# Layer-norm transposes moved from TensorE to VectorE blocks and an exchange through DRAM

## The chip, the cores and the metric

The kernel runs on one core of a Trainium2 chip. The core has five engines that work side by side, each through its own instructions in order: TensorE (PE in the profile; PEld is its weight load), VectorE (DVE), ScalarE (ACT), GpSimd (POOL) and SyncE (SP), which here only issues DMAs. An engine waits on semaphores that other engines and DMAs raise. The metric is the device time of one execution in microseconds (us), the median of several runs.

## The reference

The input is eight sequences `x` of 512 tokens and 128 features, all in float32. Three steps follow one another, each added to `x`: half an FFN of the layer-normed `x`, attention over the layer-normed `x`, half an FFN of the layer-normed `x` again, with the same FFN weights.

```python
x = x + 0.5 * ffn(layernorm(x))
x = x + attention(layernorm(x))      # 16 heads, rank 64, softmax over 512 keys, V*O folded into VO
x = x + 0.5 * ffn(layernorm(x))

def ffn(h):
    for blk in range(3):
        y = qlora_linear(h, 2 * blk)              # 128 -> 128
        y = layernorm(y) * gamma[blk] + beta[blk]
        y = gelu(y)                               # exact gelu
        h = qlora_linear(y, 2 * blk + 1) + h
    return h
```

So each sequence goes through nine layer norms over the 128 features: one in front of each FFN, three inside each FFN, and one in front of the attention. The quantized weights and their low-rank parts are folded into one 128 x 128 matrix per layer (`wT`) at the start.

## The kernel before

A tile holds one sequence as [128 tokens, 4 chunks, 128 features]. A layer norm needs its statistics along the features, so it works with tokens on partitions; the matmul behind it contracts over features, so its input must have features on partitions. Between the two lies a transpose of each 128 x 128 chunk.

The order of work is written out by hand. A function `at(t, fn)` files each step under a time on a schedule, and at the end all steps are sorted by these times and recorded; that order is then the order on each engine. The times only order the work; they are not microseconds. The schedule is cut into 32 turns (`SUP` is 32.0 units of it, about 32 us on the chip); turn `s` is numbered from 0, and each does the scores and softmax of two pairs of heads. Four turns are one sequence's attention. The FFN steps of other sequences are woven into the turns.

In a turn, `lay_turn` handles eight chunks of scores (two pairs of heads by four query chunks), numbered 0 to 7 here. For each chunk TensorE writes the scores into one of two PSUM buffers tagged `scores` (line 752), VectorE takes the row maxima (line 759, called max0 to max7 below), ScalarE takes the exponentials and their sums (line 764), VectorE the reciprocal (line 771), GpSimd divides the first head (line 776) and ScalarE the second (line 778), and VectorE turns the result in 32 x 32 blocks (line 792). When four chunks are done, 16 DMAs issued from SP (line 848) move the blocks between partition groups, 2 MB in all, into `eT`, and TensorE multiplies `eT` with the values in the next turn (line 869). Two such exchanges are issued in each turn. Since there are two score buffers, the scores of chunk n+2 wait for the exponentials of chunk n. At the end of a turn come the projections (`pqk`, line 689), the values (`pv`, line 712) and the second matmuls of the FFN blocks (`po`, line 419). All of these stand on TensorE in the written order.

A layer norm is a `Norm` object with four steps: `stats` on VectorE (lines 352 and 354), `root` on GpSimd, which raises variance plus epsilon to the power -1/2 (line 360), `scale` on VectorE, four instructions of 128 x 128 that subtract the mean and multiply with the root (line 365), and `turn`, four transposes on TensorE into a PSUM bank (line 334). ScalarE then reads that bank: `gelu` inside an FFN block (line 412), a plain copy `ffn_start` in front of an FFN (line 431) or `keep` in front of the attention (line 620). Names in the profile: `z`, `mv`, `rstd` and `p` belong to the norms in FFN blocks; with `_n` to the norm in front of an FFN, with `_an` to the one in front of the attention.

How many norms fall into a turn follows from the schedule. From turn 7 to turn 26 the pattern repeats every four turns. In turns 7, 11, 15, 19 and 23 there are three (the attention norm, a block's norm and an FFN's first norm); in the other turns of that stretch there are two. In turns 8, 10, 12 and so on (the even ones) both belong to FFN blocks; in turns 9, 13, 17, 21 and 25 one is a block's and one an FFN's first.

In each turn the three `root`s and then, from schedule time 4.0 on, the divisions of line 776 stand on GpSimd, and VectorE holds max0, max1, then the `scale`s and two reciprocals, then max2.

Of the kernel before, what the change touches and what calls it, by code (L numbers as in the profile page):

```python
# [10 lines left out]
F32 = mybir.dt.float32  # L11
I32 = mybir.dt.int32
AF = mybir.ActivationFunctionType
# [5 lines left out]
def kernel(  # L19
# [26 lines left out]
    nc = tc.nc  # L46
    B, T, D = x.shape
    H, R, _ = wq.shape
    NL = qweights.shape[0]
    NB = NL // 2  # L50
    NG = scales.shape[2]
    GROUP = D // NG
    LR = lora_a.shape[1]
    P = 128
    NC = T // P
    Q4 = P // 32
    EPS = 1e-5
    HP = H // 2
    SUP = 32.0
# [3 lines left out]
    const = ctx.enter_context(tc.tile_pool(name="const", bufs=1))  # L63
    work = ctx.enter_context(tc.tile_pool(name="work", bufs=3))
    small = ctx.enter_context(tc.tile_pool(name="small", bufs=8))

    class Psum:


        def __init__(self):  # L70
            self.names, self.stack = ["start", "attention", "end"], ExitStack()
# [34 lines left out]
    xs = [const.tile([P, NC, D], F32, name=f"x{b}") for b in range(B)]  # L106
# [7 lines left out]
    G = 3  # L114
# [1 line left out]
    qk_sb = work.tile([P, 2, HP, D], F32, tag="eT", name="qk_sb", bufs=3)  # L116
    q_sb, k_sb = qk_sb[:, 0, :, :], qk_sb[:, 1, :, :]
    sc = const.tile([P, NL, NG], F32, name="sc")
    la = [const.tile([LR, G, D], F32, name=f"la{i}") for i in range(2)]
    lb = [const.tile([P, G, LR], F32, name=f"lb{i}") for i in range(2)]  # L120
    bias_rows = const.tile([NL, D], F32, name="bias_rows")
    gb_rows = const.tile([2 * NB, D], F32, name="gb_rows")
# [16 lines left out]
    def load_projections(g0, g1):  # L139
# [24 lines left out]
        out=bias_bc,  # L164
        in_=biases.rearrange("(k two) d -> two k d", two=2)[0].partition_broadcast(P),
# [8 lines left out]
    def at(t, fn, *args):  # L174
        tasks.append((t, len(tasks), fn, args))
# [34 lines left out]


    sc75 = const.tile([P, NL, NG], F32, name="sc75")
    w = [const.tile([P, G, NG, GROUP], F32, name=f"w{i}") for i in range(2)]
    lbT = [const.tile([LR, G, P], F32, name=f"lbT{i}") for i in range(2)]
    wT = const.tile([P, NL, P], F32, name="wT")

# [122 lines left out]
    class Norm:  # L339


        def __init__(self, src, name, tag):
            self.src, self.name, self.tag = src, name, tag

        def stats(self):

# [14 lines left out]

        def scale(self):
            z = work.tile([P, NC, D], F32, tag="z", name=f"z_{self.name}")
            for c in range(self.n):
                nc.vector.tensor_scalar(  # L365
                    z[:, c, :], self.src[:, c, :], self.mv[:, c, 0:1],
                    self.rstd[:, c : c + 1],
                    ALU.subtract, ALU.mult,
                )
            self.z = z[:, : self.n, :]  # L370

        def turn(self):
            self.p = transposed(self.z, f"p_{self.name}", self.tag)


    hTs = {}

    class Block:


        def __init__(self, f, k, b, tag):
            self.k, self.b, self.tag, self.name = k, b, tag, f"{f}_{k}_{b}"

        def first(self):
            self.py = bank(f"py{self.name}", self.tag)
# [6 lines left out]
        def biased(self):  # L392
            y = work.tile([P, NC, D], F32, tag="y", name=f"y{self.name}", bufs=2)
            nc.vector.tensor_tensor(  # L394
                y, self.py, bias_bc[:, self.k, :].unsqueeze(1).to_broadcast([P, NC, D]), ALU.add
            )
            self.norm = Norm(y, self.name, self.tag)
            self.norm.stats()

        def root(self):  # L400
# [5 lines left out]
        def turn(self):  # L406
            self.norm.turn()

        def gelu(self):
            k = self.k  # L410
            self.aT = work.tile([P, NC, P], F32, tag="aT", name=f"aT{self.name}", bufs=2)
            nc.scalar.activation(
                self.aT, self.norm.p, AF.Gelu,
                bias=gb[:, NB + k : NB + k + 1], scale=gb[:, k : k + 1],
            )

# [11 lines left out]

    def ffn_start(n, f, b):
        hTs[b] = work.tile([P, NC, P], F32, tag="hT", name=f"hT{f}_{b}", bufs=3)  # L430
        nc.scalar.copy(hTs[b], n.p)

    def ffn_add(f, b, tag):
        ph = transposed(hTs[b], f"ph{f}_{b}", tag)
# [135 lines left out]
    class Unit:  # L570


        def __init__(self, f, b):
            self.f, self.b, self.tag = f, b, f"g{f}"
            self.n = Norm(xs[b], f"n{f}_{b}", self.tag)

        def lay_start(self, times, tag=None):

            if tag:
                self.tag = self.n.tag = tag  # L580
            for at_n, (fn, *args) in zip(times, (
                (self.n.stats,), (self.n.root,), (self.n.scale,), (self.n.turn,),
                (ffn_start, self.n, self.f, self.b),
            )):
                at(at_n, fn, *args)

        def lay_blocks(self, s, i, other={}):

            for k in range(NB):
                m = Block(self.f, k, self.b, self.tag)
                for x, fn in zip(other.get(("first", k)) or T_FIRST[s % 4][i], (
                    m.first, m.biased, m.root, m.scale
                )):
                    at(s * SUP + x, fn)
                s += 1  # L600
                for x, fn in zip(other.get(("second", k)) or (
                    17.65 + 0.1 * i, 22.0 + 0.1 * i, 26.0, 25.4 + 0.8 * i, 26.3 + 0.8 * i
                ), (m.turn, m.gelu, exp_again, m.second, m.add)):
                    if x:
                        at(s * SUP + x, fn)
            at(
                s * SUP + other.get("end", 31.5 if s % 4 == 0 else 28.8),
                ffn_add, self.f, self.b, self.tag,
            )


    xTs, accs = {}, {}

    def lay_attn_input(b, t):

        n = Norm(xs[b], f"an{b}", "g0")

        def keep():
            xTs[b] = work.tile([P, NC, P], F32, tag="xT", name=f"axT{b}", bufs=2)
            nc.scalar.copy(xTs[b], n.p)  # L620

        at(t - SUP + 29.3, n.stats)
        at(t + 0.2, n.root)
        at(t + 4.7, n.scale)
        at(t + 17.65, n.turn)
        at(t + 17.8, keep)


# [19 lines left out]
        ),  # L648
    )

    T_EARLY, T_LATE = (28.9, 29.7, 32.3, 35.6), (31.4, 32.0, 33.8, 36.0)
    T_FIRST = (
        (T_EARLY, None), (T_EARLY, (24.2, 25.0, 26.8, 35.5)), (None, T_EARLY),
        ((25.5, 26.5, 28.5, 35.5), T_EARLY), (T_EARLY, T_LATE),
    )
    class Pair:

# [470 lines left out]
    for b in range(B):  # L1128
        if b:
            lay_attn_input(b, (b * Q - 1) * SUP)  # L1130

        if b > 2:
            s = (b - 1) * Q - 1
            t = s * SUP
            m = Unit(0, b)
            m.lay_start((t - 5.0, t + 1.1, t + 16.58, t + 20.3, t + 20.7))
            m.lay_blocks(s, 0)

        if b < B - 1:
            s = (b + 1) * Q + 1  # L1140
            t = s * SUP
            m = Unit(1, b)
            m.lay_start((t + 0.1, t + 1.1, t + 4.7, t + 17.65, t + 17.85))
            m.lay_blocks(s, 1, {
                ("second", 1): (17.75, 21.8, None, 43.2, 43.3),
                ("first", 2): (44.4, 45.45, 46.0, 46.4),
                ("second", 2): (27.80, 27.90, None, 30.44, 32.75),
                "end": 33.56,
            } if b == B - 2 else {})
# [136 lines left out]
```

## Time and profile before

| | |
|---|---|
| median of 3 runs | 1071.47 us (1070.93 to 1071.54) |
| span of the profiled execution | 1068.9 us, 2.6 us under that median; the rest lies around the span |
| PE busy | 1053.8 us, 99% of the span |
| DVE, ACT, POOL busy | 82%, 74%, 45% |
| granted TensorE clock | 0.9 or more of full speed in every slice |
| DMA | 142.4 MB; HBM reads 5.01 MB, writes 2.10 MB |
| four transposes of one norm on TensorE | 4 x 279 ns busy; they overlap |
| `scale` on VectorE, one instruction | 356 ns (`z`), 466 ns (`z_n`), 500 ns (`z_an`) |
| division on GpSimd, 128 x 512 | 1564 ns |
| block transpose on VectorE, 128 x 1024 | 1231 ns |
| one DMA of the exchange, 128 KB | 2.3 us from issue to landing, SP spends about 0.59 us on its issue |
| store of a result, 256 KB to DRAM | 2.4 us from issue to landing |

A busy PE row says only that some matmul is in flight. The chain that ended last and the timeline of each engine tell which wait ends last; they are shown with the prediction. Idle time of VectorE, ScalarE or GpSimd counts only where that engine's result is waited for.

### The profile page before, as it was taken

Reading aid. Unit: us, or ns where it says so; the run is one execution under the profiler, and the core shown is the slowest. Engines: PE = TensorE matmul, PEld = TensorE weight load, DVE = VectorE, ACT = ScalarE, POOL = GpSimd, SP = SyncE. Lnnn points to the kernel's source line nnn. Section 1 sums busy time; section 2 is a strip of 40 time slices with the busy share of each in tenths; the row PEclk is TensorE's granted clock in tenths of the full one; section 3 lists DMA queues with packets and bytes.
Section 4 is the critical chain, followed back from the end, with each engine's and each line's share of the span. In section 5 each row is a group of like instructions: output and inputs, shape, how many; then the busy total and the mean of one; then the engine's idle time right before and its main releaser. Section 6 shows DMA issues by size and latency. Waiting matters only on the chain.

```text
span 1068.9 us, 15650 instructions
## 1 busy us (share of the span) xinstructions
PE 1053.8 (99%) x4628; PEld 560.2 (52%) x4628; DVE 873.2 (82%) x1767; ACT 793.9 (74%) x1710; POOL 485.1 (45%) x368
## 2 busy tenths in 40 slices
PE   9899999999999999999999999999999999999998
PEld 7445554545555554555545555554555554455546
DVE  6897868788888888888889888888888888777765
ACT  4877787777777787777787777787777787777742
POOL 4554434545443454444445444455444445444423
PEclk9999999999999999999999999999999999999999
DMA  6166655665576555566455566555567555566660
GB/s 189 38 141 138 158 129 132 140 141 128 120 167 158 121 117 119 129 158 158 110 130 126 122 155 155 131 124 122 117 152 167 126 125 117 131 145 158 158 158 21
DMA packets 58572, 142.40 MB, mean 133 GB/s; under 512 B 18732, under 2 KB 22904, under 8 KB 58488
## 3 DMA queue, kind: packets, MB, share of 16 engines
q1 hardware_dynamic: 56120, 139.94, 57.0%
q10 hardware_dynamic: 2368, 1.45, 0.6%
q8 instruction: 39, 0.64, 0.3%
q14 instruction: 45, 0.37, 0.1%
HBM read 5.01 MB, written 2.10 MB: 7 GB/s over the span
## 4 chain that ended last, share of the span: by engine, by line
PE 91%; DVE 3%; ACT 2%; SPq 2%; issue 1%; DMA 0%; POOL 0%; DVEq 0%; ACTq 0%; POOLq 0%
PE acc L869 37%; PE ps L752 20%; PE pqk L689 10%; PE pv L712 10%; PE po L419 4%; PE py L387 4%; PE p L334 2%; ACT e L764 2%; PE py L489 1%; SPq L848 1%; DVE tr L792 1%; DVE nm L759 1%; SPq L824 1%; PE sum L835 1%; PE p_n L334 1%; PE ph L334 1%
## 5 line engine op out<-in xcount | busy, mean ns | idle before, releaser
L776 POOL TENSOR_SCALAR e<-e,rden 128x512 f32<-128x512 f32 x257 | 399.5, 1564 | 336.1 <-DVE rden L771 336.1
L764 ACT ACTIVATE e<-ps,nm 128x512 f32<-128x512 f32 x512 | 345.0, 685 | 157.5 <-DVE nm L759 151.5
L869 PE MATMUL acc<-eT,v 64*128 64x512 f32 (+1 forms) x1756 | 457.8, 590 | 0.7 <-DMA eT<-tr 0.7
L759 DVE TENSOR_REDUCE nm<-ps 128x2 f32<-128x1024 f32 x256 | 299.6, 1206 | 47.9 <-PE ps L752 47.7
L792 DVE STREAM_TRANSPOSE tr<-e 128x1024 f32<-128x1024 f32 x252 | 307.8, 1231 | 29.9 <-POOL e L776 21.9
L869 PEld LDWEIGHTS acc<-eT,v 64*128 64x128 f32 (+1 forms) x1756 | 192.2, 187 | 216.9 <-issue 215.1
L752 PE MATMUL ps<-qk 64*128 64x512 f32 x1024 | 248.1, 598 | 2.8 <-ACT e L764 1.8
L778 ACT ACTIVATE e<-e,rden 128x512 f32<-128x512 f32 x255 | 176.0, 726 | 15.2 <-DVE rden L771 13.9
L752 PEld LDWEIGHTS ps<-qk 64*128 64x128 f32 x1024 | 94.6, 186 | 126.2 <-issue 83.3
L712 PE MATMUL pv<-vo_sb,axT 128*128 128x256 f32 x512 | 121.7, 380 | 0.3 <-ACT e L764 0.3
L712 PEld LDWEIGHTS pv<-vo_sb,axT 128*128 128x128 f32 x512 | 94.8, 190 | 28.7 <-issue 12.4
L360 POOL TENSOR_TENSOR rstd<-mv,mhalf 128x4 f32<-128x4 f32 x42 | 42.9, 1022 | 146.7 <-DVE mv L354 145.9
L764 ACT ACTIVATION_READ_ACCUMULATOR e<-ps,nm 128x1 f32 x512 | 103.6, 202 | 0.0
L725 ACT COPY v<-pv 128x512 f32<-128x512 f32 x124 | 66.8, 594 | 42.0 <-PE pv L712 42.0
L771 DVE RECIPROCAL rden<-den 128x2 f32<-128x2 f32 x256 | 41.4, 165 | 36.3 <-ACT e L764 35.4
L695 ACT COPY qk<-pqk 128x1024 f32<-128x1024 f32 x61 | 61.0, 1000 | 3.9 <-PE pqk L689 3.9
L689 PE MATMUL pqk<-axT,qT_w 128*128 128x512 f32 x122 | 63.3, 601 | 0.2 <-ACT e L764 0.2
L689 PE MATMUL pqk<-axT,kT_w 128*128 128x512 f32 x122 | 62.3, 592 | 0.0
L387 PEld LDWEIGHTS py<-wT,hT 128*128 128x128 f32 x336 | 42.3, 191 | 13.0 <-DVE hT L425 9.2
L365 DVE TENSOR_SCALAR z<-y,mv,rstd 128x128 f32<-128x128 f32 x168 | 48.1, 356 | 0.6 <-POOL rstd L360 0.6
L394 DVE TENSOR_TENSOR y<-py,bias_bc 128x512 f32<-128x512 f32 x42 | 28.7, 683 | 22.6 <-PE py L387 22.0
L387 PE MATMUL py<-wT,hT 128*128 128x128 f32 x336 | 45.4, 278 | 1.0 <-DVE hT L425 0.8
(143 smaller groups left out, 724.0 us busy)
## 6 DMA issues: line engine op xcount, KB each, us to landing
eT<-tr SPq DMA_DIRECT2D x1008, 128.0 KB, 2.3
x<-in_L_attn_x_dram SPq DMA_DIRECT2D x7, 256.0 KB, 6.0
out_dram<-x SPq DMA_DIRECT2D x7, 256.0 KB, 2.4
eT<-tr SPq DMA_DIRECT2D x16, 64.0 KB, 2.0
eT<-tr ACTq DMA_DIRECT2D x16, 64.0 KB, 2.1
qk_sb<-in_L_attn_Q_dram SPq DMA_DIRECT2D x1, 448.0 KB, 4.4
qk_sb<-in_L_attn_K_dram SPq DMA_DIRECT2D x1, 448.0 KB
x<-in_L_attn_x_dram SPq DMA_DIRECT2D x2, 128.0 KB, 2.8
```

The lines of the kernel that those rows point to most:

```text
L387: nc.tensor.matmul(self.py[:, c, :], lhsT=hTs[self.b][:, c, :], rhs=wT[:, 2 * self.k, :], start=True, stop=True,)
L689: nc.tensor.matmul(self.pg[:, i, :], lhsT=(qT_w, kT_w)[i][:, self.g, :], rhs=xTs[self.b], start=True, stop=True,)
L695: nc.scalar.copy(self.qk, self.pg)
L712: nc.tensor.matmul(p, lhsT=xTs[self.b][:, c, :], rhs=vo_sb[:, 2 * self.g : 2 * self.g + 2, :], start=True, stop=True,)
L725: nc.scalar.copy(self.v[:, c : c + NC // 2], self.pv[:, c : c + NC // 2])
L752: nc.tensor.matmul(ps[:, j, :], lhsT=self.qk[rows, 0, ts(c, P)], rhs=self.qk[rows, 1, :], start=True, stop=True,)
L759: nc.vector.tensor_reduce(self.nm[:, c, :], self.ps[c], AX.X, ALU.max, negate=True)
L764: nc.scalar.activation(e[:, j, :], self.ps[c][:, j, :], AF.Exp, bias=self.nm[:, c, j : j + 1], accum_out=self.den[:, c, j : j + 1],)
L776: nc.gpsimd.tensor_scalar(e, e, r, None, ALU.mult)
L778: nc.scalar.activation(e, e, AF.Copy, scale=r)
L792: nc.vector.transpose(self.tr[:, :, :, c, :], self.e[c].rearrange("p h (k j r) -> p j (h k) r", j=Q4, r=32),)
L869: nc.tensor.matmul(accs[self.b][i], lhsT=self.v[rows, k, j, :], rhs=self.eT[rows, :, j * NC + k, :], start=first, stop=end and (j == 1 or ...
```

## The change

Of the 63 norms of this kind, 59 take a new way; four keep the old one (both first norms and the first block's norm of the earliest work, and the last norm before the end part).

- `scale` moves from VectorE to GpSimd, as four instructions of the same shape. It is filed just behind its `root`, so that on GpSimd it stands in front of the turn's divisions.
- `turn` on TensorE goes. In its place `spread` on VectorE turns the whole [128, 512] tile in 32 x 32 blocks, one instruction, into a tile `zout` that the norms of a turn share. It stands behind the first reciprocal of the turn; for the attention norm behind the second one. All of them stand in front of max2.
- Once per turn an `Exchange` runs on SP: one DMA writes `zout` to a DRAM tile `far` (256 KB per norm), and four DMAs read it back into `zin`, one per group of 32 partitions, in pieces of 512 bytes per norm. On SP it is filed between the two exchanges of `eT` (schedule time 6.0), and its reads wait for the write to have landed. There are 30 such exchanges.
- ScalarE's three readers take `zin` in SBUF where they took a PSUM bank.
- `zout` and `zin` share a buffer of one (`zx`). To make room, the setup's `la` and `w` tiles now live in that buffer before the first exchange.

```diff
+SPREAD = (4.2, 4.3, 5.45)
 class Norm:
     def scale(self):
         z = work.tile([P, NC, D], F32, tag="z", name=f"z_{self.name}")
+        engine = nc.gpsimd if self.exchange else nc.vector
         for c in range(self.n):
-            nc.vector.tensor_scalar(
+            engine.tensor_scalar(
                 z[:, c, :], self.src[:, c, :], self.mv[:, c, 0:1],
                 self.rstd[:, c : c + 1],
                 ALU.subtract, ALU.mult,
             )
...
+    def spread(self):
+        nc.vector.transpose(
+            self.exchange.out()[:, :, self.slot, :, :],
+            self.z.rearrange("p c (j r) -> p j c r", r=32),
+        )
+
+    def turned(self):
+        if self.exchange:
+            return self.exchange.landed[:, :, self.slot, :, :].rearrange("p i c q -> p c i q")
+        return self.p.rearrange("p c (i q) -> p c i q", q=32)
+
+class Exchange:
...
+    def tile(self, name):
+        return work.tile(
+            [P, Q4, self.n, NC, 32], F32, tag="zx", name=f"{name}{self.s}", bufs=1
+        )
...
+    def run(self):
+        f = self.n * NC * 32
+        far = dram.tile([P, Q4, f], F32, tag="far", name=f"far{self.s}")
+        nc.sync.dma_start(out=far, in_=self.sent.rearrange("p j a c q -> p j (a c q)"))
+        self.landed = self.tile("zin")
+        for j in range(Q4):
+            nc.sync.dma_start(
+                out=self.landed[32 * j : 32 * (j + 1)].rearrange("p i a c q -> p i (a c q)"),
+                in_=far.rearrange("(i r) j f -> j r i f", r=32)[j],
+            )
+
+def exchange_of(s):
+    if s not in exchanges:
+        x = exchanges[s] = Exchange(s)
+        at(s * SUP + 6.0, x.run)
+    return exchanges[s]
...
 def lay_attn_input(b, t):
-    n = Norm(xs[b], f"an{b}", "g0")
+    n = Norm(xs[b], f"an{b}", "g0", exchange_of(b * HP // 2 - 1))
...
     at(t + 0.2, n.root)
-    at(t + 4.7, n.scale)
-    at(t + 17.65, n.turn)
+    at(t + 0.3, n.scale)
+    at(t + SPREAD[2], n.spread)
     at(t + 17.8, keep)
...
-T_EARLY, T_LATE = (28.9, 29.7, 32.3, 35.6), (31.4, 32.0, 33.8, 36.0)
+T_EARLY, T_LATE = (28.9, 29.7, 32.3, 32.4), (31.4, 32.0, 33.8, 33.9)
...
-    m.lay_start((t + 0.1, t + 1.1, t + 4.7, t + 17.65, t + 17.85))
+    m.lay_start((t + 0.1, t + 1.1, t + 1.2, t + SPREAD[1], t + 17.85))
```

## The prediction

> **What bounds the kernel now.** I read the page's busy shares first, then the chain that ended last, then the timelines of one period of four turns (turn 15 starts at 499.7 us, 16 at 532.0, 17 at 564.2, 18 at 595.8).
>
> ```profile
> PE 1053.8 (99%) x4628; PEld 560.2 (52%) x4628; DVE 873.2 (82%) x1767; ACT 793.9 (74%) x1710; POOL 485.1 (45%) x368
> ...
> PE 91%; DVE 3%; ACT 2%; SPq 2%; issue 1%; DMA 0%; POOL 0%; DVEq 0%; ACTq 0%; POOLq 0%
> ...
> L776 POOL TENSOR_SCALAR e<-e,rden 128x512 f32<-128x512 f32 x257 | 399.5, 1564 | 336.1 <-DVE rden L771 336.1
> L360 POOL TENSOR_TENSOR rstd<-mv,mhalf 128x4 f32<-128x4 f32 x42 | 42.9, 1022 | 146.7 <-DVE mv L354 145.9
> L365 DVE TENSOR_SCALAR z<-y,mv,rstd 128x128 f32<-128x128 f32 x168 | 48.1, 356 | 0.6 <-POOL rstd L360 0.6
> ```
>
> TensorE carries 91% of the chain: it bounds the whole. GpSimd's 336 us of idle time wait for VectorE's reciprocals, so it has room on average. What matters is when. The chain's pieces at the end of turn 16, with ScalarE's timeline there and one row of the waits:
>
> ```profile
> 549.35 1.02 PE p L334 x8
> 550.38 3.44 PE acc L869 x8
> 553.81 1.72 PE pqk L689 x4
> 555.53 1.73 PE pv L712 x8
> 557.25 1.72 PE po L419 x4
> ```
>
> ```profile
> 555.89 1.45 ACT L412 ACTIVATE aT<-p,gb 128x512 f32<-128x512 f32 x2
> ```
>
> ```profile
> PEld po L419 <- ACT aT L412: 6.8, 22, 1.0
> ```
>
> Eight transposes (two norms) hold the chain for 1.02 us. But `po` behind them needs ScalarE's gelus: the first ends near 556.67 and `po` starts at 557.25, and 22 of the `po` weight loads already wait for them. The reader is to see that TensorE can't come forward by the whole 1.02 us. Next GpSimd and VectorE at the start of turn 15 (three norms):
>
> ```profile
> 499.11 1.03 POOL L360 TENSOR_TENSOR rstd_an<-mv_an,mhalf 128x4 f32<-128x4 f32 x1 [7.31 <-DVE mv_an L354]
> 500.88 1.01 POOL L360 TENSOR_TENSOR rstd<-mv,mhalf 128x4 f32<-128x4 f32 x1 [0.73 <-DVE mv L354]
> 501.86 1.01 POOL L360 TENSOR_TENSOR rstd_n<-mv_n,mhalf 128x4 f32<-128x4 f32 x1
> 504.96 1.58 POOL L776 TENSOR_SCALAR e<-e,rden 128x512 f32<-128x512 f32 x1 [2.09 <-DVE rden L771]
> ```
>
> ```profile
> 503.68 1.11 DVE L365 TENSOR_SCALAR z<-y,mv,rstd 128x128 f32<-128x128 f32 x4
> 504.77 1.84 DVE L365 TENSOR_SCALAR z_an<-x,mv_an,rstd_an 128x128 f32<-128x128 f32 x4
> 506.24 2.33 DVE L759 TENSOR_REDUCE nm<-ps 128x2 f32<-128x1024 f32 x2
> ...
> 517.10 1.19 DVE L365 TENSOR_SCALAR z_n<-x,mv_n,rstd_n 128x128 f32<-128x128 f32 x4
> ```
>
> GpSimd's last root of the turn ends at 502.87, and max2 starts at 506.24: 3.4 us for all that is now put on GpSimd between them.
>
> **The cost of one scaling on GpSimd (c).** The trace has no such instruction there. The nearest is line 776: the same operation on 512 columns in 1.56 us with one arithmetic step and one scalar. A quarter of it is 0.39 us, the lower bound. With a fixed part of 0.19 us (GpSimd's 128x1 additions, 190 ns each) the slope is 2.68 ns a column, and 128 columns take 0.53 us. If the second arithmetic step costs as much as the first, it is 0.19 + 2 x 0.34 = 0.88 us, the upper bound. I take 0.53, as the row is the same operation and the fixed part is measured.
>
> The Trainium skill speaks against the move: GPSIMD Engine Reference, section Engine selection, says to leave elementwise work on a tile to VectorE, since GpSimd is about half as fast; its section on elementwise accounting, however, gives 769 ns for 512 one-input elements, half of the 1564 ns that this trace shows. A quarter of the page's figure would make an estimate of c = 0.19 us and, by the walk below, of 1068 us for the whole (the turns of three norms then lose 0.4 us each, the others gain 0.3); no row here shows such a speed, and the row decides.
>
> **The change part by part.**
>
> *TensorE.* 59 norms x 4 transposes leave. In the chain view one norm holds 0.44 to 0.59 us: 1.47 us in a turn of three, 1.02 for two block norms, 0.93 for a block and a first norm. Over all turns 5 x 1.47 + 11 x 1.02 + 5 x 0.93 + 3 x 1.0 + 6 x 0.5 = 29 us. How much arrives depends on the wait behind it.
>
> *VectorE.* Four scalings per norm go (1.1 to 1.9 us), one block transpose of 512 columns comes: half of 1231 ns is 0.62, the 128x512 addition takes 0.68; I take 0.64. VectorE gets lighter, but all `spread`s stand in front of max2, and a `spread` waits for GpSimd. Behind it on VectorE are queued max2 and max3, behind these ScalarE's exponentials 2 and 3, and behind these TensorE's scores 4 and 5.
>
> *Turns of three norms (7, 11, 15, 19, 23), at turn 15's times.* GpSimd does the attention root, the block's root (ends 501.89), eight scalings, the last root (1.02, and 0.1 for its own result), four scalings: it ends at 501.89 + 12 x 0.53 + 1.12 = 509.37. The first `spread` in VectorE's order takes just that last result. Three of them and a reciprocal (0.12) put max2 at 509.37 + 3 x 0.64 + 0.12 = 511.41 instead of 506.24, 5.17 later. Scores 5 had 0.8 us of air (exponentials 3 end at 510.2, TensorE reaches them at 511.07), so TensorE stalls. Of the delay, 1.1 us come back where `z_n` no longer stands in front of max6 (517.10), and 0.28 us are added by two ScalarE reads from SBUF (line 778 from SBUF 726 ns, line 725 from PSUM 594: 0.13 to 0.14 each). `po` started 0.14 us behind its gelu (ends 525.48, starts 525.62), so there is no air: it comes 5.17 - 1.1 + 0.28 = 4.35 us later. The transposes' 1.47 us vanish in that wait. Five turns: +21.8 us.
>
> *Turns with a block and a first norm (9, 13, 17, 21, 25).* At turn 17's times GpSimd starts at 564.04: root, scalings, root, scalings end at 564.04 + 1.03 + 0.1 + 2.12 + 1.02 + 0.1 + 2.12 = 570.53; one `spread` and a reciprocal later max2 is at 571.29 instead of 570.71. `po` is bound by its gelu here too, so +0.58 + 0.14 = 0.72 us; five turns: +3.6.
>
> *Turns with two block norms (2, 8, 10, ... 26, eleven).* Their statistics are ready before the turn's scores (root at 531.41 in turn 16; scalings end by 534.6, max1 only at 535.45). No delay. The gain is `po`'s air: 557.25 - 556.67 less 0.1 for the semaphore and 0.14 for the SBUF read, 0.34 us; eleven turns: -3.7.
>
> *The rest.* Turn 1 has a division in front of its second norm on GpSimd, and max2 goes from 65.47 to 68.5: +3.0. Turn 27: GpSimd ends 889.83, max2 at 891.23 instead of 889.94, +1.4 with the gelu. Turns 3, 5, 6, 28 to 31: between 0 and -0.5 each, I take -0.2: -1.4.
>
> *DMAs and SP.* 59 x 256 KB go out and come back, +30 MB to 142. The write is issued when SP has issued its last `eT` (about 506 in turn 15) and `spread` is done: 511.4. The 256 KB store lands in 2.4 us; 768 KB at the 210 GB/s that the exchange reaches take 2.5 us more: landed at 516.3. The four reads take 0.6 us of SP each, 3.7 us of moving, 2.3 us to land: about 522.3. The copy that wants them stands in front of exponentials 6, now near 523.7, so it needs them by 522.9. It just fits. In turn 17 they land near 581.5 against 582.2. In the other turns they have 4 us. On SP the next 16 issues of `eT` stand behind the reads, but their tiles are ready later still (517.1, now 522.3). So: nothing, if the reads land as the rows say. Loads of 256 KB from DRAM at the start took 4.6 us in the median (6.3 at most); at 6.3 for the last read they would be 1 to 1.5 us late in ten turns, about 12 us.
>
> *The sum.* 21.8 + 3.6 + 3.0 + 1.4 - 3.7 - 1.4 = +24.7 us on the profiled execution's 1068.9, and so on the median that stands 2.6 above it: 1071.5 + 24.7 = **1096 us**, 2.3% slower. Each 0.1 us of c moves it by 12 x 5 + 8 x 7 scalings, 11.6 us: c = 0.39 gives 1080, c = 0.88 gives 1137.
>
> **The rivals.**
>
> *Two steps cost double on GpSimd* (c near 0.88): the same waits, longer: 1137 us (1120 to 1145). For it: one `root` of only four columns takes 1.02 us, so arithmetic isn't cheap there. Against: a power is no multiplication.
>
> *The data come late through DRAM.* The forecast plus 12 us: 1108. For it: the copy in front of exponentials 6 has half a microsecond of air. Against: DMA engines are idle from 507 to 517 us.
>
> *TensorE's saving arrives in full, and the kernel is faster.* If the gelu's chain can be shifted with TensorE, 29 us come off. Against it stand the late max2s, counted on TensorE alone: 5 x (5.17 - 0.5) + 2.5 + 0.8 = 26.7 us at c = 0.53, so 1069; at c = 0.39, 10.6 less, 1059. It decides from c of about 0.53 downwards. For it: 91% of the chain is TensorE's. Against: `po` already waits for its gelus. I give 1064.
>
> **How the numbers follow.** The forecast with c between 0.45 and 0.65 (1088 to 1110) gets 0.58; the lower end, c near 0.39 (1078 to 1086), 0.08; doubled cost 0.12; late data 0.10; TensorE's saving in full 0.12, of which 0.09 faster and 0.03 within 0.2%, which is about what a measurement can tell from no change here. So slower has 0.88. The range leaves out the faster part and the upper half of the doubled cost: 1072 to 1130.
>
> **What would show it.** Right: in turns 7, 11, 15, 19 and 23 VectorE's block transpose of `z` idles some 4 to 5 us for GpSimd's scaling, max2 comes 5 us late and TensorE's scores 4 and 5 wait for ScalarE; `po` waits more for `aT`; scalings on GpSimd near 0.53 us; TensorE's idle time rises from near nothing to over 40 us. Wrong: scalings under 0.3 us, `spread`s that never wait, or readers of `zin` that wait for DMAs. I would be wrong most of all by the price of that one instruction, or if ScalarE's chain to the gelu isn't as rigid as I read it.

## The result and the profile after

| | before | after |
|---|---|---|
| median | 1071.36 us (1070.93 to 1071.54, 4 runs) | 1132.92 us (1131.36 to 1133.40, 4 runs) |
| ratio, 95% interval | | 1.0573 (1.0558 to 1.0588) |
| span of the profiled execution | 1068.9 us | 1131.6 us |
| DMA | 142.4 MB | 173.3 MB |

The changed kernel is 5.7% slower; 1096 us was forecast, with 1130 us as the upper end. The direction was right, the size was not, and the range missed the time by 3 us. Line numbers in what follows are those of the changed kernel: the division of line 776 is now line 846, the scaling 372, the spread 383, scores 822, exponentials 834, the block's gelu 476, `po` 483.

From the page of the changed kernel, three parts: busy time of the engines, the chain by engine, and the group of the moved scaling (its busy time, mean ns of one, idle time before).

```profile
PE 1057.8 (93%) x4392; PEld 540.7 (48%) x4392; DVE 845.8 (75%) x1590; ACT 793.1 (70%) x1710; POOL 668.0 (59%) x604
...
PE 50%; DVE 14%; POOL 12%; ACT 10%; SPq 7%; issue 4%; DMA 3%; DVEq 0%; ACTq 0%; POOLq 0%
...
L372 POOL TENSOR_SCALAR z<-y,mv,rstd 128x128 f32<-128x128 f32 x160 | 124.8, 793 | 3.6
```

TensorE held 91% of the chain before and holds 50% now; GpSimd went from nothing to 12%. And c, the price that the forecast hung on, is 0.793 us, not 0.53. The waits of the changed kernel (us in total, times, longest):

```profile
DVE zout L383 <- POOL z_n L372: 58.0, 12, 8.5
...
PE ps L822 <- ACT e L834: 50.9, 25, 6.8
...
DVE zout L383 <- POOL z L372: 15.1, 5, 4.3
...
PE po L483 <- ACT aT L476: 6.7, 20, 0.7
```

The first line is the step that was foretold: VectorE's block transpose idles for GpSimd's last scaling, up to 8.5 us at a time. The second is what it does to TensorE. The same wait in the kernel before, under that kernel's line numbers:

```profile
PE ps L752 <- ACT e L764: 1.8, 3, 0.7
```

The start of turn 15 (526.74 us; it was at 499.64), GpSimd's timeline, VectorE's and TensorE's:

```profile
527.98 1.01 POOL L366 TENSOR_TENSOR rstd<-mv,mhalf 128x4 f32<-128x4 f32 x1 [0.74 <-DVE mv L360]
528.98 3.12 POOL L372 TENSOR_SCALAR z_an<-x,mv_an,rstd_an 128x128 f32<-128x128 f32 x4
532.09 3.12 POOL L372 TENSOR_SCALAR z<-y,mv,rstd 128x128 f32<-128x128 f32 x4
535.17 1.02 POOL L366 TENSOR_TENSOR rstd_n<-mv_n,mhalf 128x4 f32<-128x4 f32 x1
536.30 3.12 POOL L372 TENSOR_SCALAR z_n<-x,mv_n,rstd_n 128x128 f32<-128x128 f32 x4
```

```profile
539.45 0.71 DVE L383 STREAM_TRANSPOSE zout<-z_n 128x512 f32<-128x512 f32 x1 [8.52 <-POOL z_n L372]
...
540.72 0.69 DVE L383 STREAM_TRANSPOSE zout<-z_an 128x512 f32<-128x512 f32 x1
541.33 2.32 DVE L829 TENSOR_REDUCE nm<-ps 128x2 f32<-128x1024 f32 x2
```

```profile
533.71 3.60 PE L939 MATMUL acc<-eT,v 64*128 64x512 f32 x16
544.11 3.79 PE L822 MATMUL ps<-qk 64*128 64x512 f32 x8 [6.80 <-ACT e L834]
```

The reader is to see one queue: twelve scalings at 0.78 us each, with a root between them, end at 539.4; three spreads follow; max2 starts 14.6 us into the turn instead of 6.6; TensorE stands still for 6.8 us and only then does scores 4.

Since TensorE's order is the same in both kernels but for the transposes, the turns can be compared one by one, from the first score matmul of a turn to that of the next:

| turns | forecast | measured |
|---|---|---|
| 7, 11, 15, 19, 23 (three norms) | +4.35 each, +21.8 | +6.28, +8.61, +7.63, +7.14, +8.60: +38.3 |
| 9, 13, 17, 21, 25 (block and first norm) | +0.72 each, +3.6 | +2.43 each: +12.2 |
| 8, 10, ... 26 and 2 (two block norms) | -0.34 each, -3.7 | -0.22 to -0.32 each in ten, turn 2 +1.27: -1.2 |
| 1 | +3.0 | +5.0 |
| 27 | +1.4 | +3.6 |
| 3, 5, 6, 28 to 31 | -1.4 | +4.4 (turn 3 +1.8, turn 31 +2.4) |
| start and turns 0, 4 | 0 | +0.5 |
| sum | +24.7 | +62.7, the difference of the spans |

### The profile page after: what moved, and what is told of

It reads as the page before. It is cut to its first block, busy times and chain, and to the rows that moved or that the text cites. A ratio compares the mean times of both kernels' runs of the same rounds, so it can differ in the third digit from the quotient of the medians.

```text
span 1131.6 us, 15586 instructions
## 1 busy us (share of the span) xinstructions
PE 1057.8 (93%) x4392; PEld 540.7 (48%) x4392; DVE 845.8 (75%) x1590; ACT 793.1 (70%) x1710; POOL 668.0 (59%) x604
## 4 chain that ended last, share of the span: by engine, by line
PE 50%; DVE 14%; POOL 12%; ACT 10%; SPq 7%; issue 4%; DMA 3%; DVEq 0%; ACTq 0%; POOLq 0%
PE acc L939 18%; PE ps L822 12%; PE pqk L759 6%; SPq L918 6%; ACT e L834 6%; DVE tr L862 5%; POOL z L372 4%; DVE nm L829 4%; PE pv L782 4%; PE po L483 3%; DMA eT<-tr 3%; POOL z_n L372 3%; PE py L448 2%; ACT L476 2%; POOL z_an L372 2%
## 5 line engine op out<-in xcount | busy, mean ns | idle before, releaser
L846 POOL TENSOR_SCALAR e<-e,rden 128x512 f32<-128x512 f32 x257 | 398.9, 1563 | 243.9 <-DVE rden L841 243.5
L939 PE MATMUL acc<-eT,v 64*128 64x512 f32 (+1 forms) x1756 | 463.8, 595 | 0.6 <-DMA eT<-tr 0.6
L862 DVE STREAM_TRANSPOSE tr<-e 128x1024 f32<-128x1024 f32 x252 | 307.7, 1231 | 29.5 <-POOL e L846 19.3
L822 PE MATMUL ps<-qk 64*128 64x512 f32 x1024 | 263.8, 625 | 52.4 <-ACT e L834 50.9
L939 PEld LDWEIGHTS acc<-eT,v 64*128 64x128 f32 (+1 forms) x1756 | 195.6, 189 | 242.5 <-issue 239.1
L372 POOL TENSOR_SCALAR z<-y,mv,rstd 128x128 f32<-128x128 f32 x160 | 124.8, 793 | 3.6
L841 DVE RECIPROCAL rden<-den 128x2 f32<-128x2 f32 x256 | 37.2, 145 | 44.0 <-ACT e L834 43.0
L383 DVE STREAM_TRANSPOSE zout<-z_n 128x512 f32<-128x512 f32 x12 | 8.5, 712 | 58.0 <-POOL z_n L372 58.0
L483 PE MATMUL po<-aT,wT 128*128 128x512 f32 x84 | 43.3, 621 | 6.8 <-ACT aT L476 6.7
```

Of the source, the lines that this page charges most:

```text
L372: engine.tensor_scalar(z[:, c, :], self.src[:, c, :], self.mv[:, c, 0:1], self.rstd[:, c : c + 1], ALU.subtract, ALU.mult,)
L483: nc.tensor.matmul(self.po, lhsT=wT[:, 2 * self.k + 1, :], rhs=self.aT, start=True, stop=True)
L822: nc.tensor.matmul(ps[:, j, :], lhsT=self.qk[rows, 0, ts(c, P)], rhs=self.qk[rows, 1, :], start=True, stop=True,)
L846: nc.gpsimd.tensor_scalar(e, e, r, None, ALU.mult)
L862: nc.vector.transpose(self.tr[:, :, :, c, :], self.e[c].rearrange("p h (k j r) -> p j (h k) r", j=Q4, r=32),)
L939: nc.tensor.matmul(accs[self.b][i], lhsT=self.v[rows, k, j, :], rhs=self.eT[rows, :, j * NC + k, :], start=first, stop=end and (j == 1 or ...
```

## The experiments

Ratios are against the kernel before in the same comparison, whose median there was 1070.99 to 1071.29 us. Where an edit adds or removes lines, the line numbers of that run are shifted by some.

### One arithmetic step in the scaling

```diff
-            engine = nc.gpsimd if self.exchange else nc.vector
             for c in range(self.n):
-                engine.tensor_scalar(
+                if self.exchange:
+                    nc.gpsimd.tensor_scalar(
+                        z[:, c, :], self.src[:, c, :], self.rstd[:, c : c + 1], None, ALU.mult
+                    )
+                    continue
+                nc.vector.tensor_scalar(
...
```

> The changed kernel with the scaling on GpSimd reduced to one arithmetic step (times the root; the subtraction of the mean is left out, so its results differ from the reference's). Theory A (the second arithmetic step is what c was short of, and c alone sets the size of the loss): one scaling takes about 0.53 us instead of 0.793, and by the sum's slope of 11.6 us per 0.1 us the time falls from 1132.9 to about 1102 us (1096 to 1108). Rival B (the price is a fixed cost of the instruction, whatever its steps): the scaling stays at 0.75 to 0.80 us, the time within 3 us of 1133. Rival C (the lower bound, a quarter of the long row): 0.39 us and 1086 us.

Measured: 1104.47 us, ratio 1.0314 (1.0299 to 1.0330). GpSimd's groups of this run:

```profile
L850 POOL TENSOR_SCALAR e<-e,rden 128x512 f32<-128x512 f32 x257 | 398.7, 1563 | 259.4 <-DVE rden L845 259.3
L372 POOL TENSOR_SCALAR z<-y,rstd 128x128 f32<-128x128 f32 x160 | 93.8, 604 | 3.3
```

The time lies in theory A's band: the second step, with its operand, costs 0.19 us of the 0.79. But the one-step scaling takes 0.604, not the 0.53 that was interpolated. A straight line through the two rows has (1563 - 604) / 384 = 2.5 ns a column and 0.28 us fixed, against the 0.19 us borrowed from an addition of one column. The median fell by 28.4 us for 0.189 us, 15.0 us per 0.1 us; the sum had 11.6. Between the two profiled executions lie 29.5 us: turns 1, 2, 3 and 27, which the slope left out, give 5.9 of them, turn 31 gives 2.1 (more on it below), the two groups of turns that it counted 20.5.

### Scaling alone on GpSimd, the turn still on TensorE

```diff
+            engine = nc.gpsimd if self.far else nc.vector
             for c in range(self.n):
-                nc.vector.tensor_scalar(
+                engine.tensor_scalar(
...
```

(`far` marks the same 59 norms; their scalings are filed at the changed kernel's times)

> The kernel before with the scaling alone moved to GpSimd, at the places that the changed kernel gives it; the turn stays on TensorE at its old place, there is no spread and no trip through DRAM. Theory A (what hurts is that GpSimd's queue ends 7.5 us later in the turns of three norms; without the spread the next in line are its divisions and VectorE's transposes of e in front of max4): VectorE's first transpose of e comes near 514 instead of 509.4 in turn 15, max4 5 us late, less 1.1 us for z_n that leaves VectorE: about +4 us in each of five turns, +0.5 in the five turns of a block and a first norm, +5 in turns 1 and 27: 1095 to 1101 us. Rival B (only the spread in front of max2 hurts): 1069 to 1074 us. Rival C (GpSimd's price counts in full whoever waits, and TensorE's transposes are still there): 1130 to 1140 us.

Measured: 1108.54 us, ratio 1.0348 (1.0332 to 1.0363). The turns of three norms lose 5.4 to 6.9 us without a single spread, those of a block and a first norm 0.54, those of two blocks nothing. VectorE's and TensorE's timelines of this run in turn 15, which starts at 513.30 us:

```profile
527.60 1.25 DVE L794 STREAM_TRANSPOSE tr<-e 128x1024 f32<-128x1024 f32 x1 [5.01 <-POOL e L778]
...
530.31 2.32 DVE L761 TENSOR_REDUCE nm<-ps 128x2 f32<-128x1024 f32 x2
```

```profile
533.09 3.79 PE L754 MATMUL ps<-qk 64*128 64x512 f32 x8 [4.07 <-ACT e L766]
```

Theory A's mechanism: the divisions now stand behind the twelve scalings, the transposes of `e` wait for the divisions, and max4 stands behind these, 17.0 us into the turn instead of 12.1. The time is 7.5 us above the band: the turns lose more than the 4 us expected, and turn 31 is 2.4 us longer. A part is TensorE's clock (see TensorE kept busy, below): the eight scores take 3.79 us here too, and turns 15 and 23, with 6.83 us at half clock, lose 6.8 to 6.9 us, the other three, with 3.41 us, 5.4 to 5.8. So a later place for the spreads alone would not have saved these turns: GpSimd's own divisions stand behind the same queue.

### Scaling back on VectorE, the rest as changed

```diff
-            engine = nc.gpsimd if self.exchange else nc.vector
+            engine = nc.vector
```

(with the scalings filed at about their old times, but `z_n`, which stood in front of max6, now with the others in front of the spreads and max2)

> The changed kernel with the scaling put back on VectorE in front of the spreads, at about its old places; spread and the trip through DRAM as changed. Theory A (in the turns of three norms VectorE itself is on the path, so z_n's 1.2 us and three spreads of 0.65 in front of max2 still cost 2.7 us a turn; 1.2 in the turns of a block and a first norm, about 0.3 in those of two blocks, some 5 us in turns 1 to 3 and 27): 1092 to 1102 us, as one scaling on GpSimd at 0.5 us would. Rival B (GpSimd alone makes the loss, VectorE has room for the spreads): 1065 to 1072 us.

Measured: 1097.88 us, ratio 1.0253 (1.0237 to 1.0268), inside theory A's band. Turns of three norms +2.0 to +2.9 us, of a block and a first norm +1.1 to +1.5, of two blocks +0.15 to +0.31. GpSimd is thus not the only trouble: in this run's turn 15 VectorE works without a gap from 516.00 us until max2 starts at 521.69, 9.7 us into the turn instead of 6.6. It has no room in front of max2 for three spreads (0.67 to 0.71 us each) and `z_n`'s scaling (1.28 us) either.

### The first norm's scaling moved into GpSimd's idle time

```diff
-            m.lay_start((t - 5.0, t + 1.1, t + 1.2, t + SPREAD[0], t + 20.7))
+            m.lay_start((t - 5.0, t - 3.9, t - 3.8, t + SPREAD[0], t + 20.7))
```

> The changed kernel with the root and the scaling of the first norm of an FFN filed 5 units of the schedule earlier in the five turns of three norms (its statistics are ready 4 us before the turn), so that on GpSimd they fall into its idle time at the end of the turn before, and eight scalings instead of twelve stand between the turn's start and max2. Theory A (the delay is the length of GpSimd's queue in front of max2, whatever stands in it): the queue ends about 4 us earlier, max2 comes 4.5 us earlier, and these turns lose 2 to 3.5 us instead of 7.7: 1105 to 1113 us. Rival B (the wait is set by something else, the late root of the block's norm or the spreads' order): 1125 us or more.

Measured: 1109.75 us, ratio 1.0360 (1.0343 to 1.0377), 23 us under the changed kernel. The five turns lose 2.1 to 3.2 us instead of 6.3 to 8.6; all others are as in the changed kernel within 0.2 us, but for the start and turn 31. VectorE's timeline of this run in turn 15, which starts at 518.66 us:

```profile
522.91 0.71 DVE L383 STREAM_TRANSPOSE zout<-z_n 128x512 f32<-128x512 f32 x1
527.52 0.71 DVE L383 STREAM_TRANSPOSE zout<-z 128x512 f32<-128x512 f32 x1 [3.90 <-POOL z L372]
```

Four scalings out of the queue in front of max2, and 3.90 us of waiting instead of 8.52. The queue's length is the cause, as theory A has it.

### Without the trip through DRAM

```diff
-            f = self.n * NC * 32
-            far = dram.tile([P, Q4, f], F32, tag="far", name=f"far{self.s}")
-            nc.sync.dma_start(out=far, in_=self.sent.rearrange("p j a c q -> p j (a c q)"))
-            self.landed = self.tile("zin")
-            for j in range(Q4):
-                nc.sync.dma_start(
-                    out=self.landed[32 * j : 32 * (j + 1)].rearrange("p i a c q -> p i (a c q)"),
-                    in_=far.rearrange("(i r) j f -> j r i f", r=32)[j],
-                )
+            self.landed = self.sent
```

> The changed kernel without the trip through DRAM: ScalarE's readers take zout itself, so the blocks stay in their partition groups and the results differ from the reference's; all else is as it is. Theory A (the data land in time everywhere, the trip costs nothing but the 2.4 us by which the last transfers of eT come later in turn 31): 1129 to 1133 us. Rival B (the prediction's second: data late in the turns with little air): 1118 to 1124 us.

Measured: 1133.57 us, ratio 1.0589 (1.0573 to 1.0604); the changed kernel stands at 1.0573. The time is 0.6 us above theory A's band, but not shorter than with the trip: the trip costs nothing that shows. In the changed kernel's turn 15 the four reads are issued between 544.75 and 546.5 us and land 2.8 to 4.5 us after their issue, so by 551.0, and the first reader starts at 552.02. In the whole trace ScalarE never stands idle in front of a reader of `zin`. My aside on turn 31 fell: it is 3.1 us longer here too, with no trip at all.

### TensorE kept busy while it waits

```diff
+        if s in (7, 11, 15, 19, 23):
+            def fill():
+                p = bank(f"fill{s}", "g0")
+                for i in range(13):
+                    nc.tensor.matmul(p, lhsT=ident, rhs=vo_sb[:, 0:4, :], start=True, stop=True)
+            at(t + 9.5, fill)
```

(In a second run `range(6)`.) The windows of the changed kernel show why. A row has the window in us and its length, then busy time and instructions of PE, PEld, DVE, ACT and POOL, the granted clock (1.00 is full speed), and the DMAs' share and GB/s:

```profile
540.00:544.00 4.00, 0.00 (x0) 0.00 (x0) 3.65 (x6) 2.11 (x6) 2.51 (x2) 0.67 0.45 183
544.00:548.00 4.00, 3.89 (x10) 1.79 (x12) 3.67 (x6) 2.62 (x7) 3.10 (x2) 0.50 0.60 150
```

Behind 6.8 us without a matmul the granted clock is 0.50, and eight score matmuls take 3.79 us where they took 1.88; from 548 to 552 us it is 0.98 again.

> The changed kernel with 13 matmuls of 128 x 512 on constants in front of scores 4 in the five turns of three norms, about 5.6 us of work that nobody reads, where TensorE stood idle for 5.9 to 6.8 us. Theory A (part of the loss is the granted clock, which the windows show at 0.50 for some 4 us behind this idle time, so that eight score matmuls take 3.8 us instead of 1.9): with TensorE kept busy the scores take 1.9 us and each of the five turns gets 1.0 to 2.5 us shorter: 1120 to 1128 us. Rival B (the low clock there is hidden behind VectorE and ScalarE, which have their own work to catch up with): 1130 to 1135 us.

Measured: 1145.68 us, ratio 1.0692 (1.0676 to 1.0708). A miss of my own making: 13 matmuls took 11.43 us, not 5.6, and held up the scores themselves; each of the five turns lost 10.1 us. It tells nothing on the clock's share. With six:

> The changed kernel with 6 instead of 13 of these matmuls in the five turns of three norms. The 13 took 11.4 us (each goes through TensorE twice, 0.43 us a pass) and held the scores by themselves; six take 5.2 us and end some 1.7 us before scores 4 can start. Theory A (the low clock behind the idle time is a part of the loss): scores 4 and 5 take 1.9 us instead of 3.8 at the same start, and these turns lose 5.2 to 5.8 us instead of 6.3 to 8.6: 1121 to 1126 us. Rival B (VectorE and ScalarE hide the low clock): 1130 to 1135 us.

Measured: 1126.40 us, ratio 1.0512 (1.0496 to 1.0528). TensorE's timeline of this run in turn 15:

```profile
535.96 5.42 PE L1049 MATMUL fill<-vo_sb,ident 128*128 128x512 f32 x12
542.88 1.13 PE L822 MATMUL ps<-qk 64*128 64x512 f32 x4 [1.51 <-ACT e L834]
544.22 1.13 PE L822 MATMUL ps<-qk 64*128 64x512 f32 x4 [0.21 <-ACT e L834]
```

The clock stays at 1.00 in the windows from 540 to 548 us and the scores take 1.1 us for four. The five turns lose 6.0 to 6.9 us, together 4.7 us less than in the changed kernel. The median fell by 6.5 us; in the profiled execution turn 31 alone is 3.0 us shorter, and turn 1 is 1.3 us longer. So the low clock is a part of the loss, about 0.9 us a turn on average, less than theory A had (the time is just above its band). In the changed kernel TensorE works 3.1 to 6.0 us of these turns at half clock, 4.4 on average, which stretches that work by 2.2 us; more than half of this is hidden behind other engines. Two runs without a filler show a like price. With the scaling on VectorE, turns 7 and 19 have 3.41 us at half clock and lose 2.9 us, while 11, 15 and 23 have none and lose 2.0. With the first norm's scaling moved, turn 7 has none and loses 2.1, the other four have 3.41 us each and lose 3.1 to 3.2.

### The gelu in front of the last divisions

```diff
-                    17.65 + 0.1 * i, 22.0 + 0.1 * i, 26.0, 25.4 + 0.8 * i, 26.3 + 0.8 * i
+                    17.65 + 0.1 * i, 20.6 + 0.01 * i, 26.0, 25.4 + 0.8 * i, 26.3 + 0.8 * i
```

> The changed kernel with the block norms' gelu one place earlier on ScalarE: in front of the last two divisions (line 848, 1.51 us the pair) instead of behind them. Theory A (TensorE's saving is stopped by the gelu alone, as the prediction's third rival needs): the gelus end 1.5 us earlier, the wait of po for aT goes, and each of 21 turns with block norms gets 0.7 to 1.0 us shorter: 1112 to 1118 us; the turns of two block norms go from 31.5 to 32.0 us to about 31. Rival B (the two divisions pushed back by 2.8 us delay VectorE's last block transposes, the FFN additions behind them and so the next block's matmuls): 1131 to 1140 us.

Measured: 1148.68 us, ratio 1.0726 (1.0709 to 1.0744), outside both bands. Against the changed kernel, turns 8, 12, 16, 20, 24 and 26 (two block norms) get 0.2 us shorter still, turns 10, 14, 18 and 22 of the same kind 0.9 longer, those of a block and a first norm 1.3 longer. VectorE's and TensorE's timelines at the end of turn 14 of this run:

```profile
528.81 2.37 DVE L862 STREAM_TRANSPOSE tr<-e 128x1024 f32<-128x1024 f32 x2 [2.92 <-ACT e L848]
531.11 0.71 DVE L489 SCALAR_TENSOR_TENSOR hT<-po,cols,hT 128x512 f32<-128x512 f32 x1
```

```profile
528.32 1.88 PE L483 MATMUL po<-aT,wT 128*128 128x512 f32 x4
...
533.57 1.16 PE L448 MATMUL py<-wT,hT 128*128 128x128 f32 x8 [0.89 <-DVE hT L489]
```

`po` no longer waits (0.34 us in the changed kernel), but VectorE's transposes of `e` wait 2.92 us for the divisions, the FFN addition stands behind them, and the next `py` waits 0.89 us for the addition. Rival B's mechanism, at a higher price than it named: over the whole trace these transposes wait 68.5 us for ScalarE's divisions, 27 times.

### The change in ten turns only, and a new order at their end

```diff
+    FAR = range(8, 27, 2)
...
-                far = s > -1 and not (("second", k) in other and self.f and k == NB - 1)
+                far = s + 1 in FAR
...
```

(the other norms go back to the kernel before, with their times)

> The change only where it gained by the comparison of turns: in the ten even turns from 8 to 26, whose two norms both belong to blocks (20 norms); all others keep VectorE's scaling and TensorE's transposes. Theory A (each turn stands for itself: these ten got 0.23 to 0.32 us shorter each, and the loss sits in the others): 2.5 us under the kernel before, 1068.3 to 1069.3 us. Rival B (the late turns before them gave these turns the time for their scaling and trip, and without them the exchange or GpSimd is late here as well): 1071 us or more.

Measured: 1069.44 us, ratio 0.9980 (0.9971 to 0.9989). Each of the ten turns gains what it gained in the changed kernel (0.22 to 0.31 us) and all others stand within 0.1 us, but for turn 31 (+0.4). The median is 0.1 us above the band of theory A, and 0.2% under the kernel before, with the interval below 1.

The new order, in the turns named by `ORDER` (in the next two runs the same ten turns):

```diff
-                    17.65 + 0.1 * i, 22.0 + 0.1 * i, 26.0, 25.4 + 0.8 * i, 26.3 + 0.8 * i
+                    17.65 + 0.1 * i, 20.6 + 0.01 * i if s in ORDER else 22.0 + 0.1 * i, 26.0, 25.4 + 0.8 * i, 26.3 + 0.8 * i
...
+            if s in ORDER and x > 5:
+                ta = 25.4 + 0.05 * (x - 6)
...
+            if s in ORDER and x > 5:
+                u = 27.2 + 0.05 * (x - 6)
...
-            at(t + (24.5 if s % 4 != 3 else 27.2), two[1].exchange)
+            at(t + (27.3 if s in ORDER else 24.5 if s % 4 != 3 else 27.2), two[1].exchange)
```

The first pair moves the gelus, `ta` ScalarE's last divisions behind the copies, `u` VectorE's last transposes of `e` behind the additions, and the last pair the second exchange of `eT` behind these.

> The kernel of the ten turns with the end of these turns in another order: on ScalarE the gelus stand in front of the last two divisions, and these behind the copies of qk and v; on VectorE the last two transposes of e stand behind the FFN additions, so that nothing on TensorE's path waits for them. Theory A (TensorE's saving of 0.93 us per turn arrives once neither the gelu nor the additions hold it): 0.7 to 0.9 us per turn instead of 0.25, 1062 to 1065 us. Rival B (the late transposes of e now hold the next turn's first maxima or its statistics on VectorE): 1069 us or more.

Measured: 1067.13 us, ratio 0.9961 (0.9949 to 0.9974). The time lies between the two bands. The ten turns gain 0.83 to 0.92 us each, as theory A had it, but the turns of three norms behind turns 10, 14, 18 and 22 lose 0.80 to 0.88 us. In these VectorE is on the path: its late transposes of `e` push the statistics and the first maxima, as rival B feared for all (max0 starts 2.7 us into turn 15, without the new order 1.2 us).

> The kernel before with the same new order at the end of the same ten turns and nothing else, the control: its transposes stay on TensorE. If the new order is worth nothing by itself, since po there starts 0.1 us behind its gelu anyway: 1070 to 1072 us. If the order is what brings the time, and the norms' turn nothing: as fast as the run with both, 1062 to 1066 us.

Measured: 1074.41 us, ratio 1.0026 (1.0016 to 1.0036), above both bands. The order alone gives nothing in the ten turns (0.00 to -0.04 us) and costs the same 0.8 to 0.9 us in four turns of three norms. So the order by itself gains nothing; what the run with both gains has the size of TensorE's own saving, and is that saving, let through.

> The kernel of the ten turns with the new order at the end of only six of them (8, 12, 16, 20, 24 and 26), since in the run with ten the turns of three norms behind turns 10, 14, 18 and 22 got 0.8 to 0.9 us longer. If each turn stands for itself: 6 x 0.6 us under the kernel of the ten turns without the new order, 1065 to 1066.5 us. If the loss of 0.88 us moves to other turns: 1067 us or more.

Measured: 1065.11 us, ratio 0.9947 (0.9934 to 0.9959): 6 us under the kernel before and the fastest that was run. TensorE's timeline at the end of turn 16 of the changed kernel, then of this one:

```profile
589.27 1.89 PE L782 MATMUL pv<-vo_sb,axT 128*128 128x256 f32 x8
591.49 1.98 PE L483 MATMUL po<-aT,wT 128*128 128x512 f32 x4 [0.34 <-ACT aT L476]
```

```profile
552.15 1.89 PE L786 MATMUL pv<-vo_sb,axT 128*128 128x256 f32 x8
553.88 1.88 PE L485 MATMUL po<-aT,wT 128*128 128x512 f32 x4
```

With the gelus early and nothing behind them on the path, `po` follows `pv` at once.

## Why the prediction was wrong

*The bound and the mechanism: right.* TensorE was the bound, GpSimd's place in the turn decided, and the wait arose at the spread in front of max2 and went on through the exponentials to scores 4 and 5, in the turns that were named.

*c: the step that failed.* 0.793 us instead of 0.53. Two errors lie in it, by the one-step run: the fixed part is 0.28, not 0.19 us, if a straight line holds (with the slope a little lower, 0.07 of the 0.26 us that were missing), and the second arithmetic step with its operand costs 0.19 us where the forecast took it for free. Put into the forecast's own sum, 0.793 gives GpSimd's end at 501.89 + 12 x 0.793 + 1.12 = 512.53 and max2 at 514.57, 8.33 late, +7.5 us for a turn of three norms (measured 7.65 in the mean), +2.8 for a block and a first norm (2.43), and 2.1 more in turns 1 and 27 each, so 5.1 and 3.5 (5.0 and 3.6). The whole is then +55 us, 1127 us: 30 of the 37 us that were missing are this one price. That the single turns fit so closely is in part luck: max2 came 8.0 us late, not 8.33, and some 0.9 us of a turn's 7.65 are the low clock, which the sum didn't have. The doubled-cost rival, which I gave 12%, named 1137 us and was the nearest, though the second step does not cost as much as the first (0.19 us against 0.32, which is 128 columns at 2.5 ns).

*The page's price.* The Trainium skill, GPSIMD Engine Reference, would have made c an estimated 0.19 us by the best case in its section on elementwise accounting; the trace has four times that. Its section Engine selection names half of VectorE's speed for operations with two inputs alone, which the prediction left out, and "roughly line-rate" for one. The scaling has one tensor as its input, and took 793 ns against VectorE's 356 to 500: the measurement decides.

*The slope was too flat.* 11.6 us per 0.1 us of c counted twelve scalings in five turns and eight in seven. Turns 2 and 3, taken as turns without a delay, have their second statistics late as well, and lost 1.3 and 1.8 us.

*The spread:* 0.64 us estimated, 0.69 to 0.71 measured. Three of them in front of max2 make 0.2 us a turn.

*Turns of two block norms: right in ten of eleven.* The gain is `po`'s air, forecast 0.34, measured 0.22 to 0.32 us. The size is in part luck, since two errors cancel. The price of a SBUF read was overestimated: the gelu takes 809 ns from `zin` and 777 from PSUM, 0.03 instead of 0.14 us. And the air was read from two views: the chain has `po` at 557.25, the timeline, from which the gelu's end was taken, at 557.09.

*DMAs: right.* The data were in time, with more air than the forecast gave them, because the copy that wants them came later still; the run without the trip shows it.

*TensorE's saving in full:* it did not come, but the reason was only half seen. `po`'s wait for the gelu does stop it; taking that wait away alone made things worse, because the divisions behind the gelu feed VectorE's transposes and these stand in front of the FFN additions. With both moved, 0.83 to 0.92 us arrive in a turn of two block norms. The eight transposes there take 0.93 us of TensorE's timeline in the kernel before (from 549.28 to the next matmul at 550.21 in turn 16); the chain view, which the forecast used, has 1.02.

*The clock was not in the sum at all.* The forecast reckoned waits in TensorE time at full speed; the low clock costs some 0.9 us in each turn of three norms, and in the profiled execution 1.4 of turn 31's 2.4 us (see the end).

## What to carry to other kernels

When work moves to an idle engine, price the very instruction (its steps, its size), not its nearest relative, and count the queue that it makes in front of the next thing that somebody waits for; idle time of that engine on average says nothing. A gain on the bounding engine arrives only as far as the next wait behind it: look which one ends last, and what stands behind the instructions that are moved to shorten it. A change that loses on the whole may gain in one kind of stage; the table of turns shows which, and there it can be kept.

## What the runs showed of the hardware

GpSimd's `tensor_scalar` on fp32 with one scalar per partition takes 604 ns for 128 columns and 1563 ns for 512 with one step, 793 ns for 128 columns with two steps; VectorE took 356 to 500 ns for the same two-step work in the kernel before.

The granted TensorE clock halves behind a stretch in which TensorE did little, and which waits it catches is partly chance. In each trace it changes only at times that lie whole multiples of 3.413 us apart. In the changed kernel it falls at 264.86, 401.39, 541.34, 677.87 and 814.41 us, which are 40, 41, 40 and 40 such steps, and stays at 0.50 for two or three steps. Cut into these steps, TensorE's busy times in the 14 traces of this case give a sharp border: behind a step at full clock in which TensorE was busy for less than 41% of the time, the next step has 0.50; behind busier ones it doesn't, but for the last step of two runs. Once low, the clock stayed low behind steps busy for up to 80%, and was full again behind 85% and more. So a wait of 2.55 us is enough if it falls well, as in turn 31 of the changed kernel, where TensorE waits for the last blocks of `eT`:

```profile
1097.72:1101.13 3.41, 1.34 (x4) 0.27 (x2) 2.80 (x13) 0.00 (x0) 1.03 (x1) 1.00 0.84 204
1101.13:1104.54 3.41, 2.93 (x7) 2.43 (x8) 0.41 (x2) 0.00 (x0) 0.00 (x0) 0.50 0.24 59
```

TensorE was busy for 1.34 of 3.41 us, and the ten `sum` matmuls behind took 3.84 us. In the kernel before the wait there was 1.56 us, no step was low, and they took 2.40 us. The four runs with a low step over this work have a turn 31 that is 2.3 to 3.1 us longer than before, the nine others -0.6 to +0.7 us, whatever their change. The five turns of three norms differ in the same way: in the changed kernel those with two low steps lost 6.3 to 7.6 us, those with three 8.6; with none, TensorE kept busy, they lost 6.0 to 6.9.

The Trainium skill, TensorE: Matmul & The Clock Gate, section What's actually happening, gives such a rule: half rate after an idle window of about 3.4 us, in a window that runs freely, so that the moment varies. The steps of 3.413 us agree with it; that the window has to be idle does not, since 39% of work was not enough here.
